# Products of 64 rows or columns made 128 wide, and the shared experts of four sequences moved beside the routed ones

## The chip, the cores and the metric

The kernel runs on one core of a Trainium2 chip. The metric is device time in microseconds (us) of one launch. The engines are PE (TensorE; its weight loads are listed as PEld), DVE (VectorE), ACT (ScalarE), POOL (GpSimd), and SP, whose queue issues most DMA transfers; POOL issues the indirect ones (gathers and scatter-adds by a list of row numbers). Each engine works through its own instructions in the order in which they were written; across engines they wait for each other by semaphores.

## The reference, cut to what matters

Two layers over 8 sequences of 512 tokens with 256 features, all in fp32; each adds its result to its input.

```python
# layer 0: an adapter per sequence (weights by language), then experts that choose tokens
h = relu(hidden @ W1[lang] + b1[lang])                 # 256 -> 64
c0 = layernorm(hidden + h @ W2[lang] + b2[lang]) * gamma[lang] + beta[lang]
G, I = top_k(swapaxes(softmax(c0 @ Wg.T)), 128)        # each of 8 experts takes 128 tokens a sequence
x = x + scatter_add(I, G * (gelu(c0[I] @ W1e + b1e) @ W2e + b2e))      # 256 -> 1024 -> 256

# layer 1: conditioning by running averages, then 64 routed experts and a shared one
md = 0.5 + sigmoid(gelu(x @ Wn1.T + bn1) @ Wn2.T + bn2)                # 256 -> 64 -> 8
c1 = layernorm((gelu(x @ Wsoma.T + ..) * sigmoid(traces(x, md) @ Wtemp.T + ..)) @ Wout.T) * gamma + beta
w, ids = top_k(softmax(c1 @ router_w.T), 8)            # of 64 experts; the first 128 tokens of each count
routed = segment_sum(w * ((silu(xe @ w_gate) * (xe @ w_up)) @ w_down)) # 256 -> 192 -> 256
sg, su = split(c1 @ ws_gate_up)                        # 192 and 192 columns
shared = (silu(sg) * su) @ ws_down
x = x + routed + shared
```

## The kernel before

**An order written by a planner.** The program is not written engine by engine. Functions add *steps* to an `Order` (L39): an engine, a planned cost in us, a function that issues the instructions, what it reads and writes, buffers that it takes from a ring (`new`), and a rank. `run` (L102) plays the steps through with the planned costs: on each engine it takes, of the steps that can begin within 0.25 us of the earliest one, that with the lowest rank. The order in which it takes them is the order in which the instructions are issued. Loads and stores are steps of SP with 0.1 us and a size; the planner lets them finish one behind the other at `RATE` = 0.19e6 bytes per us, and 2 us later. `after` holds a step back in the plan until others are done. The planned costs are no times of the chip; waits on the chip come from the tiles that instructions share.

**The stages.** `adapter(b)` (L300) for 8 sequences; `down` multiplies by the 64 columns of the gathered `aw1` (L354). `choose` makes the token lists of layer 0 on DVE. `expert(n)` (L582, down to the scatter-adds of L728) runs 8 experts for each of 4 groups of two sequences: `up` (L643), `down` (L710), then scatter-adds into `x1_rows`. `conditioning(b)` (L824) needs all experts of its group; in it `hidden` (L849) has 64 output columns and `rates` (L858) 64 rows and 8 columns, the scans are DVE's (L969, L980). `route` and `last_lists` make the token lists of the routed experts on DVE. These stages overlap: experts (rank 1000 + n) fill PE around the conditioning (rank 100 + 5 b).

**The shared experts.** `shared(b)` (L1266, rank 2000 + b, so it fills what is left of PE) reads the normed sequence back (`rc1b`, one buffer), makes gate and up in four products of 96 columns (`CH`), two at a time (L1287), multiplies silu of the one by the other (L1296 on ACT, L1299 on DVE) into `rsh`, multiplies by `wsd` in two halves of 96 rows (L1313), copies to `rob` (L1318) and stores that into `odd`, a DRAM tensor (L1326).

**The routed experts.** `pair(p)` (L1331) loads the weights of two experts, 1152 KB, into one of 6 `wfar` or 8 `wnear` buffers; pair p takes over the place of pair p - 14. `routed(e)` (L1342, rank 400 + e): a gather of 128 tokens on POOL (L1351), two transposes (L1360), scale (ACT), gate and up in one product of 384 columns (L1371), silu (L1374), a multiply (L1377), two transposes of the 192 columns (L1386; the two blocks of 128 overlap by 64), a copy (L1389), the down product as one of 128 rows (L1396) and one of 64 (L1397), a copy (L1400), and a scatter-add on POOL (L1403) into `out` for even e, into `odd` for odd e. Adds into one tensor follow each other, each waits for the landing of the one before. An add into `odd` waits for the shared sums of all eight sequences, which are stored there first; `out` holds the residual.

**The final sums.** `total(b)` (L1422) loads `odd` and `out`, adds on DVE and stores.

Each fp32 product appears as two MATMUL records.

Of the kernel before, what the change touches and what calls it, by code (L numbers as in the profile page):

```python
# [26 lines left out]
CH = 96  # L27
PAIR = 2 * 2 * (H // P) * F1 + 3 * H
FAR = 6
NEAR = 8  # L30
# [8 lines left out]
class Order:  # L39
# [3 lines left out]
    RATE = 0.19e6  # L43
# [101 lines left out]
def kernel(ctx: ExitStack, tc: tile.TileContext, d: dict, out: bass.AP):  # L145
# [64 lines left out]
        "rlr": 2, "rtk": 1, "rm8": 2, "rev": 1, "rhalf": 1, "rsecond": 1, "rws": 1, "rc1b": 1, "rsh": 1, "rsl": 1, "rob": 1,  # L210

        "wfar": FAR, "wnear": NEAR, "xe": 6, "xeT": 3, "xsl": 2, "xhe": 2, "xheT": 2, "xye": 4,
# [87 lines left out]
    def adapter(b):  # L300
# [19 lines left out]
        def row_w1():  # L320
            t = tile_of(w1, "aw1", [P, NH, A])
            nc.gpsimd.indirect_dma_start(
                out=t.rearrange("p c a -> p (c a)"), out_offset=None, in_=d["cw1"],
                in_offset=bass.IndirectOffsetOnAxis(ap=ix_w1[:, b : b + 1], axis=0),
            )
# [20 lines left out]
        pool(1.1, row_w1, new=[(w1, "aw1")], rank=rank, lag=2.5)  # L346
        pool(1.1, row_w2, new=[(w2, "aw2")], rank=rank, lag=2.5)
        pool(1.0, one, new=[(hT, "ahT")], rank=rank)
        pool(1.1, row_gains, w=[("gains", b)], rank=rank, lag=2.5)

        def down():
            ph = bank(("ph", b))
            for hc in range(NH):
                nc.tensor.matmul(ph[:A, :], V[w1][:, hc, :], V[xb][:, hc, :], start=hc == 0, stop=hc == NH - 1)  # L354
# [385 lines left out]
    def w_load():  # L740
# [14 lines left out]
        one("wn2", [HN, D1], d["wn2"], 2 * KB)  # L755
        one("bn1", [HN, 1], d["bn1"], 256)
        one_w("wn1", H, HN)
# [6 lines left out]
        one("wsd", [CH, 2, H], d["wsd"].rearrange("(c p) n -> p c n", p=CH), 192 * KB)  # L764
# [59 lines left out]
    def conditioning(b):  # L824
# [20 lines left out]
        def hidden():  # L845
            pn = bank(("pn", b))
            tile_of(K["hn"], "hn", [HN, S])
            for hc in range(NH):
                nc.tensor.matmul(  # L849
                    pn[:HN, :], W["wn1"][:, hc, :], V[K["xb"]][:, hc, :], start=hc == 0, stop=hc == NH - 1  # L850
                )

        def hidden_gelu():
            nc.scalar.activation(V[K["hn"]], V["pn", b][:HN, :], AF.Gelu, bias=W["bn1"])

        def rates():
            tile_of(K["md"], "md", [D1, S])
            nc.tensor.matmul(bank(("pm", b))[:D1, :], W["wn2"], V[K["hn"]], start=True, stop=True)  # L858
# [406 lines left out]

    def shared(b):  # L1266
        rank, soon = 2000 + b, 250 + b
        c1T, sh, ob = ("c1b", b), ("sh", b), ("ob", b)
# [6 lines left out]
        for f in range(2):  # L1275
            banks = [("sgu", b, f, k) for k in range(2)]
            sl = ("sl", b, f)
            for k in range(2):
                def into(f=f, k=k, banks=banks, sl=sl):
                    if k == 0:  # L1280
                        tile_of(sl, "rsl", [CH, S])
                        if f == 0:
                            tile_of(sh, "rsh", [CH, 2, S])
                    t = bank(banks[k], "hid")
                    f0 = k * F1 + f * CH
                    for hc in range(NH):
                        nc.tensor.matmul(  # L1287
                            t[:CH, :], W["wsgu"][:, hc, f0 : f0 + CH], V[c1T][:, hc, :],
                            start=hc == 0, stop=hc == NH - 1,
                        )  # L1290

                new = [(banks[k], "hid")] + ([(sl, "rsl")] if k == 0 else []) + ([(sh, "rsh")] if f + k == 0 else [])
                lead = [pe(2.0, into, r=[c1T, "wsgu"], new=new, rank=rank, after=lead if f + k else ())]

            def silu(banks=banks, sl=sl):
                nc.scalar.activation(V[sl], V[banks[0]][:CH, :], AF.Silu)  # L1296

            def mul(f=f, banks=banks, sl=sl):
                nc.vector.tensor_tensor(V[sh][:, f, :], V[sl], V[banks[1]][:CH, :], ALU.mult)  # L1299

            act(0.65, silu, r=[banks[0]], w=[sl], rank=soon, table="s")
            dve(0.75, mul, r=[sl, banks[1]], w=[sh], rank=45)
        for h in range(NC // 2):
            po = ("spo", b, h)

            def down(h=h, po=po):
                if h == 0:
                    tile_of(ob, "rob", [P, NC, H])
                t = bank(po, "hid").rearrange("p (c h) -> p c h", h=H)
                for c in range(2):  # L1310
                    tok = (2 * h + c) * P
                    for f in range(2):
                        nc.tensor.matmul(  # L1313
                            t[:, c, :], V[sh][:, f, tok : tok + P], W["wsd"][:, f, :], start=f == 0, stop=f == 1
# [5 lines left out]
            new = [(po, "hid")] + ([(ob, "rob")] if h == 0 else [])  # L1320
            lead = [pe(2.0, down, r=[sh, "wsd"], new=new, rank=rank, after=lead if h else ())]
            act(0.65, keep, r=[po], w=[ob], rank=soon)

        def store():

            nc.sync.dma_start(out=odd[b * S : (b + 1) * S, :].rearrange("(c p) h -> p c h", p=P), in_=V[ob])  # L1326

        load(512 * KB, store, r=[ob], w=[("sum", 1, b)], rank=rank)
# [12 lines left out]

    def routed(e):  # L1342
        rank = 400 + e
        j = e % 2
        wp_, xe, xeT, sl, he, heT, ye = (("pair", e // 2), *((k, e) for k in ("xe", "xeT", "xsl", "xhe", "xheT", "xye")))
# [20 lines left out]
        def gate_up():  # L1366
            tile_of(sl, "xsl", [P, F1])
            tile_of(he, "xhe", [P, F1])
# [7 lines left out]
        def mul():  # L1376
            nc.vector.scalar_tensor_tensor(  # L1377
                V[he], V[pgu][:, F1 : 2 * F1], V[xe][:, H + e : H + e + 1], V[sl], ALU.mult, ALU.mult
# [3 lines left out]
        def turn_h():  # L1382
            tile_of(heT, "xheT", [P, 2, C1])
            t = bank(pt)
            for f in range(2):
                nc.tensor.transpose(t[:, f * P : (f + 1) * P], V[he][:, f * (F1 - P) : f * (F1 - P) + P], ident)  # L1386
# [4 lines left out]

        def down():
            tile_of(ye, "xye", [P, H])
            t = bank(po, "res")[:, :H]
            rest = slice(P // 2, P) if j else slice(0, P // 2)
            nc.tensor.matmul(t, V[heT][:, 1 - j, :], wdn(j), start=True, stop=False)  # L1396
            nc.tensor.matmul(t, V[heT][rest, j, :], wdn(2)[rest, :], start=False, stop=True)  # L1397
# [14 lines left out]
        pe(1.6, gate_up, r=[xeT, wp_], new=[(pgu, "hid"), (sl, "xsl"), (he, "xhe")], rank=rank)  # L1412
# [4 lines left out]
        pe(1.1, down, r=[heT, wp_], new=[(po, "res"), (ye, "xye")], rank=rank)  # L1417
# [4 lines left out]
    def total(b):  # L1422
        t = ("both", b)
        rows = slice(b * S, (b + 1) * S)
        part = lambda j: V[t][:, j * NC * H : (j + 1) * NC * H]

        def get_odd():
            tile_of(t, "wfar" if b < FAR else "wnear", [P, PAIR])
            nc.sync.dma_start(out=part(1), in_=odd[rows, :].rearrange("(p c) h -> p (c h)", c=NC))  # L1429

        def get():
            nc.sync.dma_start(out=part(0), in_=out[rows, :].rearrange("(p c) h -> p (c h)", c=NC))
# [4 lines left out]
        def put():  # L1437
            nc.sync.dma_start(out=out[rows, :].rearrange("(p c) h -> p (c h)", c=NC), in_=part(0))

        load(300 * KB, get_odd, r=[("chain", 1)], new=[(t, "wfar" if b < FAR else "wnear")], rank=600 + b)  # L1440
        load(300 * KB, get, r=[("chain", 0)], w=[t], rank=610 + b)
        dve(1.3, both, w=[t], rank=600)
        load(300 * KB, put, r=[t], rank=620 + b)
# [28 lines left out]
    for p in range(E1 // 2):  # L1472
        pair(p)
    for e in range(E1):
# [8 lines left out]
def layout(inputs):  # L1483
# [4 lines left out]
    w1 = a["L0_cond_W1"].reshape(NL, NH, P, A).transpose(0, 2, 1, 3).reshape(NL * P, NH * A)  # L1488
# [10 lines left out]
    rest = np.concatenate([wdn[:, 0, : F1 - P], wdn[:, 1, P:]], axis=1)  # L1499
    wpair = np.concatenate([wgu, wdn[:, 0, F1 - P :], wdn[:, 1, :P], rest], axis=2)  # L1500
# [5 lines left out]
        "cw1": w1,  # L1506
# [11 lines left out]
        "wn1": a["L1_cond_Wn1"].T,  # L1518
        "bn1": a["L1_cond_bn1"].reshape(HN, 1),
        "wn2": a["cond_256"].T,  # L1520
# [32 lines left out]
```

## Time and profile before

| | us |
|---|---|
| median of 3 runs | 1205.87 (1204.51 to 1207.83) |
| the profiled execution | 1206.65 |
| its span, first to last instruction | 1204.9 |
| PE busy | 1068.5 (89%), 4293 products |
| DVE busy | 701.2 (58%) |
| ACT busy | 469.9 (39%) |
| POOL busy | 377.3 (31%) |
| DMA moved | 221.35 MB, 184 GB/s on average |

How to read it: the busy shares are averages over stages with different limits. The page divides the span into 40 equal slices and prints the busy share of each as a digit; the timeline lists instructions in order, merged where one line follows itself ("x4"), with start, length, and in brackets the engine's idle time before and what ended it; the windows give busy times for chosen stretches. A line number is that of the listing. A matmul's length includes the filling of the array, so the distance between the starts of two records says more of its price than its length. In the names `xe<-c_rows,ix_c` stands for "written from", and buffer numbers are left out.

### The profile page before, as it was taken

What the parts mean: (1) busy time and instruction counts of PE and PEld (TensorE: products, weight loads), DVE (VectorE), ACT (ScalarE), POOL (GpSimd) and SP (SyncE); (2) the same over time, 40 slices, a digit from 0 to 9 for tenths busy, and PEclk for the clock granted to TensorE, in tenths of its full rate; (3) what the DMA queues carried; (4) which work ended last, traced back from release to release, by engine and by line L of the source; (5) the groups of instructions that cost most, each with busy time, mean ns of one, the idle gap of its engine ahead of it and who ended that gap; (6) DMA issues with size and microseconds to landing.
All of it is one profiled execution on the core that took longest, in us unless ns stands there. A gap on an engine that the chain in (4) does not pass through costs nothing. (4 is left out here: it accounts for less than half of the span.)

```text
span 1204.9 us, 12973 instructions
## 1 busy us (share of the span) xinstructions
PE 1068.5 (89%) x4293; PEld 738.1 (61%) x4293; DVE 701.2 (58%) x1486; ACT 469.9 (39%) x998; POOL 377.3 (31%) x299
## 2 busy tenths in 40 slices
PE   4779999999999999999999999899967888899950
PEld 2457888858778667878586876345543444445530
DVE  2623180059883998946997939798575223333323
ACT  2447644443536442536434544323322212223310
POOL 6132133314232213223122221000003356778850
PEclk9669999999999999999999999999978989999985
DMA  8845466755665646557755634732193478895559
GB/s 286 285 150 184 131 194 201 204 180 175 202 196 156 209 145 210 173 140 217 227 152 162 195 91 142 295 106 70 56 371 117 129 215 230 241 245 96 90 95 386
DMA packets 89443, 221.35 MB, mean 184 GB/s; under 512 B 15185, under 2 KB 62329, under 8 KB 76961
## 3 DMA queue, kind: packets, MB, share of 16 engines
q1 hardware_dynamic: 62848, 182.73, 43.6%
q0 software_dynamic: 25472, 36.75, 16.7%
q10 hardware_dynamic: 1056, 1.05, 0.3%
q8 instruction: 34, 0.56, 0.2%
q14 instruction: 33, 0.26, 0.1%
HBM read 177.24 MB, written 47.32 MB: 186 GB/s over the span
## 5 line engine op out<-in xcount | busy, mean ns | idle before, releaser
L643 PE MATMUL hid<-exT,fw 128*128 128x256 f32 x1024 | 231.5, 381 | 1.8 <-ACT hf L653 1.8
L710 PE MATMUL res<-fw,hf 128*128 128x256 f32 x1024 | 232.6, 379 | 0.0
L643 PEld LDWEIGHTS hid<-exT,fw 128*128 128x128 f32 x1024 | 193.3, 191 | 33.4 <-issue 5.3
L710 PEld LDWEIGHTS res<-fw,hf 128*128 128x128 f32 x1024 | 191.6, 190 | 24.9 <-issue 0.5
L728 POOL DMA_INDIRECT x_rows<-y,ix x64 | 113.9, 1780 | 230.4 <-ACT y L725 219.5
L609 POOL DMA_INDIRECT xg<-c_rows,ix x64 | 68.8, 1075 | 257.1 <-PE hid L622 227.1
L653 ACT ACTIVATE hf<-hid,fb 128x256 f32<-128x256 f32 x256 | 105.1, 470 | 82.0 <-PE hid L643 81.7
L1351 POOL DMA_INDIRECT xe<-c_rows,ix_c x64 | 63.0, 984 | 202.2 <-DMA c_rows<-rlr 177.9
L980 DVE TENSOR_TENSOR_SCAN t<-alpha,u 128x512 f32<-128x512 f32 x84 | 102.8, 1224 | 2.9
L969 DVE SCALAR_TENSOR_TENSOR u<-gx,blend,mdb 128x512 f32<-128x512 f32 x128 | 95.2, 744 | 1.9 <-DMA mdb<-md_rows 0.9
L725 ACT ACTIVATE y<-y,gT 128x256 f32<-128x256 f32 x64 | 31.6, 506 | 147.8 <-DVE y L722 146.5
L1400 DVE COPY xye<-res 128x256 f32<-128x256 f32 x64 | 27.2, 425 | 81.6 <-PE res L1397 38.9
L1287 PE MATMUL hid<-rc1b,wsgu 128*96 128x512 f32 x128 | 63.3, 636 | 12.3 <-DMA rc1b<-c1T_rows 12.3
L1374 ACT ACTIVATE xsl<-hid 128x192 f32<-128x192 f32 x64 | 21.1, 330 | 128.4 <-PE hid L1371 128.4
L722 DVE TENSOR_TENSOR y<-res,fb 128x256 f32<-128x256 f32 x64 | 26.1, 418 | 69.7 <-PE res L710 69.7
L1403 POOL DMA_INDIRECT odd<-xye,ix_c x32 | 50.7, 1584 | 35.1 <-DMA odd<-rob 14.3
L982 DVE TENSOR_TENSOR tmp<-tmp,t 128x512 f32<-128x512 f32 x84 | 58.1, 692 | 2.9
L1403 POOL DMA_INDIRECT out_dram<-xye,ix_c x32 | 50.8, 1588 | 27.1 <-DVE xye L1400 9.4
L278 ACT ACTIVATE xeT<-mm,lgb 128x128 f32<-128x128 f32 x128 | 48.4, 456 | 27.8 <-PE mm L1360 25.5
L278 ACT ACTIVATE exT<-hid,gains 128x128 f32<-128x128 f32 x128 | 48.0, 457 | 28.6 <-PE hid L622 28.6
L1377 DVE SCALAR_TENSOR_TENSOR xhe<-hid,xe,xsl 128x192 f32<-128x192 f32 x64 | 26.4, 413 | 41.8 <-ACT xsl L1374 34.8
L1371 PE MATMUL hid<-wnear,xeT 128*128 128x384 f32 x128 | 50.2, 518 | 0.0
(200 smaller groups left out, 1588.3 us busy)
## 6 DMA issues: line engine op xcount, KB each, us to landing
fw<-in_fw_dram SPq DMA_DIRECT2D x64, 1024.0 KB
wfar<-in_wpair_dram SPq DMA_DIRECT2D x16, 1152.0 KB
wnear<-in_wpair_dram SPq DMA_DIRECT2D x16, 1152.0 KB
mdb<-md_rows SPq DMA_DIRECT2D x32, 512.0 KB
axb<-in_xT_dram SPq DMA_DIRECT2D x8, 512.0 KB
fb<-in_fb_dram SPq DMA_DIRECT2D x32, 128.0 KB
x_rows<-axt SPq DMA_DIRECT2D x8, 512.0 KB
c_rows<-ac SPq DMA_DIRECT2D x8, 512.0 KB
```

What stands on the lines that cost most here:

```text
L278: nc.scalar.activation(dst, src, AF.Identity, bias=gain[:, NH + hc : NH + hc + 1], scale=gain[:, hc : hc + 1])
L609: nc.gpsimd.indirect_dma_start(out=tile_of(("xg", u, b), "xg", [P, H]), out_offset=None, in_=c0_rows[b], in_offset=bass.IndirectOffsetOnAx ...
L643: nc.tensor.matmul(t[:, i, :], V[w1][:, hc, f * P : (f + 1) * P], V[exT][:, hc, :], start=hc == 0, stop=hc == NH - 1,)
L653: nc.scalar.activation(t[:, i, :], p[:, i, :], AF.Gelu_apprx_tanh, bias=fb1[:, e, f : f + 1])
L710: nc.tensor.matmul(V[res][:, :H], V[hf][:, i, j * K0 : (j + 1) * K0], V[w2][:, f, :], start=f == 0, stop=f == NF - 1,)
L728: nc.gpsimd.indirect_dma_start(out=x1_rows[b], out_offset=bass.IndirectOffsetOnAxis(ap=lists[b][0][:, e : e + 1], axis=0), in_=V[y], in_of ...
L969: nc.vector.scalar_tensor_tensor(u, V[K["gx"]][:, hc, :], W["blend"][:, hc, k : k + 1], V[mdb][:, k % 2, :], ALU.mult, ALU.mult,)
L980: nc.vector.tensor_tensor_scan(t, decay(1 + k), u, 0.0, ALU.mult, ALU.add)
L982: nc.vector.tensor_tensor(whole, whole, t, ALU.add)
L1287: nc.tensor.matmul(t[:CH, :], W["wsgu"][:, hc, f0 : f0 + CH], V[c1T][:, hc, :], start=hc == 0, stop=hc == NH - 1,)
L1351: nc.gpsimd.indirect_dma_start(out=tile_of(xe, "xe", [P, H + E1]), out_offset=None, in_=c1_rows, in_offset=bass.IndirectOffsetOnAxis(ap=ix ...
L1403: nc.gpsimd.indirect_dma_start(out=odd if j else out, out_offset=bass.IndirectOffsetOnAxis(ap=ix_c1[:, e : e + 1], axis=0), in_=V[ye], in_ ...
```

## The change

Five things, and the order that the planner makes of them.

1. *128 columns or rows.* The gathered adapter weight has a third block, a copy of the first, so that the product takes 128 columns, of which rows 64 to 127 of the result aren't used. `wn1`, `bn1`, `wn2` are padded with zeros to 128. In the routed experts the hidden tile is 256 wide, with 64 zero columns behind the 192 (even e) or ahead of them (odd e); four such tiles are kept and zeroed once (`hidden_places`), and the block of `w_down` that an expert shares with its partner holds the 64 rows of both.
2. *Shared experts in three blocks.* The 384 columns of gate and up are laid out anew as 128 of gate, 128 of up, and the last 64 of both together: three products of 128 columns for four of 96. The hidden tile `sh` is one tile for all sequences, its second half 64 zero rows and 64 used ones.
3. *Four sequences later.* For b in `LATE` (4 to 7) the place in `odd` is stored with zeros, by a step that reads nothing; the down product may come only after all of `conditioning`, its result stays in SBUF (`xob`, four buffers) and is added in `total`.
4. *Buffers.* `NEAR` 8 to 6 (so 12 pairs), `rc1b` 1 to 2, `xhe` 2 to 4.
5. *Numbers of the planner.* `RATE` 0.19e6 to 0.3e6; ranks of the adapter's gathers: weights 3 lower, gains 2 higher; 0.95 for 1.1 for the routed down product.

```diff
-NEAR = 8
+NEAR = 6
+LATE = (4, 5, 6, 7)
-    RATE = 0.19e6
+    RATE = 0.3e6
...
-            t = tile_of(w1, "aw1", [P, NH, A])
+            t = tile_of(w1, "aw1", [P, NH + 1, A])
...
-        pool(1.1, row_w1, new=[(w1, "aw1")], rank=rank, lag=2.5)
-        pool(1.1, row_w2, new=[(w2, "aw2")], rank=rank, lag=2.5)
+        pool(1.1, row_w1, new=[(w1, "aw1")], rank=rank - 3, lag=2.5)
+        pool(1.1, row_w2, new=[(w2, "aw2")], rank=rank - 3, lag=2.5)
         pool(1.0, one, new=[(hT, "ahT")], rank=rank)
-        pool(1.1, row_gains, w=[("gains", b)], rank=rank, lag=2.5)
+        pool(1.1, row_gains, w=[("gains", b)], rank=rank + 2, lag=2.5)
...
-                nc.tensor.matmul(ph[:A, :], V[w1][:, hc, :], V[xb][:, hc, :], start=hc == 0, stop=hc == NH - 1)
+                nc.tensor.matmul(ph, V[w1][:, hc : hc + 2, :].rearrange("p c a -> p (c a)"), V[xb][:, hc, :], start=hc == 0, stop=hc == NH - 1)
...
-                    pn[:HN, :], W["wn1"][:, hc, :], V[K["xb"]][:, hc, :], start=hc == 0, stop=hc == NH - 1
+                    pn, W["wn1"][:, hc, :], V[K["xb"]][:, hc, :], start=hc == 0, stop=hc == NH - 1
...
-            nc.tensor.matmul(bank(("pm", b))[:D1, :], W["wn2"], V[K["hn"]], start=True, stop=True)
+            nc.tensor.matmul(bank(("pm", b)), W["wn2"], V[K["hn"]], start=True, stop=True)
...
+    REST = slice(2 * P - F1, P)
+    sh = pools["pr"].tile([P, 2, S], F32, name="sh", bufs=1)
+    nc.gpsimd.memset(sh[: 2 * P - F1, 1, :], 0.0)
+    zeros = const.tile([P, H], F32, name="zeros")
+    nc.gpsimd.memset(zeros, 0.0)
...
+        banks = [("sgu", b, k) for k in range(3)]
+        for k in range(3):
...
+                    nc.tensor.matmul(
+                        t, W["wsgu"][:, hc, k * P : (k + 1) * P], V[c1T][:, hc, :], start=hc == 0, stop=hc == NH - 1
+                    )
+            def silu(k=k, sl=sl):
+                if k:
+                    nc.scalar.activation(V[sl][REST, :], V[banks[2]][: F1 - P, :], AF.Silu)
+                else:
+                    nc.scalar.activation(V[sl], V[banks[0]], AF.Silu)
+            def mul(k=k, sl=sl):
+                at = slice(0, P) if k == 1 else REST
+                nc.vector.tensor_tensor(sh[at, k - 1, :], V[sl][at, :], V[banks[k]][at, :], ALU.mult)
+            new = [(banks[k], "hid")] + ([(sl, "rsl")] if k != 1 else [])
+            lead = [pe(2.0, into, r=[c1T, "wsgu"], new=new, rank=rank, after=lead if k else ())]
+            if k != 1:
+                act(0.65, silu, r=[banks[k]], w=[sl], rank=soon, table="s")
+            if k:
+                dve(0.75, mul, r=[sl, banks[k]], w=[("sh", k - 1)], rank=45)
...
-            lead = [pe(2.0, down, r=[sh, "wsd"], new=new, rank=rank, after=lead if h else ())]
+            lead = [pe(2.0, down, r=[("sh", 0), ("sh", 1), "wsd"], new=new, rank=rank, after=(lead if h else last_tokens if b in LATE else ()))]
...
-            nc.sync.dma_start(out=odd[b * S : (b + 1) * S, :].rearrange("(c p) h -> p c h", p=P), in_=V[ob])
-        load(512 * KB, store, r=[ob], w=[("sum", 1, b)], rank=rank)
+            src = zeros.unsqueeze(1).to_broadcast([P, NC, H]) if b in LATE else V[ob]
+            nc.sync.dma_start(out=odd[b * S : (b + 1) * S, :].rearrange("(c p) h -> p c h", p=P), in_=src)
+        load(512 * KB, store, r=() if b in LATE else [ob], w=[("sum", 1, b)], rank=80 if b in LATE else rank)
...
+    def hidden_places():
+        def fill():
+            for k in range(4):
+                t = V["he", k] = tile_of(("he", k), "xhe", [P, 2 * P])
+                nc.gpsimd.memset(t[:, F1:] if k % 2 == 0 else t[:, : 2 * P - F1], 0.0)
+        pool(1.0, fill, w=[("he", k) for k in range(4)], rank=399, after=last_tokens)
...
-                nc.tensor.transpose(t[:, f * P : (f + 1) * P], V[he][:, f * (F1 - P) : f * (F1 - P) + P], ident)
+                nc.tensor.transpose(t[:, f * P : (f + 1) * P], V[he][:, f * P : (f + 1) * P], ident)
...
-            rest = slice(P // 2, P) if j else slice(0, P // 2)
-            nc.tensor.matmul(t, V[heT][:, 1 - j, :], wdn(j), start=True, stop=False)
-            nc.tensor.matmul(t, V[heT][rest, j, :], wdn(2)[rest, :], start=False, stop=True)
+            nc.tensor.matmul(t, V[heT][:, j, :], wdn(j), start=True, stop=False)
+            nc.tensor.matmul(t, V[heT][:, 1 - j, :], wdn(2), start=False, stop=True)
...
+        laid = lambda x: x[rows, :].rearrange("(c p) h -> p c h" if b in LATE else "(p c) h -> p c h", **as_laid)
+        def shared_too():
+            nc.vector.tensor_add(part(1), part(1), V["ob", b])
...
+        load(300 * KB, get_odd, r=[("chain", 1)], new=[(t, "wfar" if b < FAR else "wnear")], w=[(t, 1)], rank=600 + b)
+        if b in LATE:
+            dve(1.3, shared_too, r=[("ob", b)], w=[(t, 1)], rank=600)
+        load(300 * KB, get, r=[t, ("chain", 0)], w=[(t, 0)], rank=610 + b)
+        dve(1.3, both, r=[(t, 1)], w=[(t, 0)], rank=600)
+        load(300 * KB, put, r=[(t, 0), t], rank=620 + b)
```

## The prediction

> **What bounds the kernel now.** I read the busy slices first, then the timeline of POOL and of PE over the routed experts, the chain of waits, and the windows. The slices:
>
> ```profile
> PE   4779999999999999999999999899967888899950
> POOL 6132133314232213223122221000003356778850
> ```
>
> One digit is 30.1 us. PE is at 9 from 90 to about 745 us (dense experts mixed with the conditioning of sequences 0 to 5); then DVE carries the conditioning of 6 and 7 (to 877) and the last token lists (to 917); from 917.64 (first gather of L1351) to the last scatter-add at 1167.04 come the 64 routed experts, where POOL climbs to 8; the last 35 us are the final sums, with PE and POOL idle. In 90 to 745 all waits of PE add up to 15.7 us (L1017 6.4, L909 3.1, xr 2.8, L643 1.8, L1113 1.6), so there PE sets the pace.
>
> The routed experts, steady part, PE and POOL timelines (start, us, group; in brackets the idle time before it and what ended it):
>
> ```profile
> 1106.56 0.59 PE L1396 MATMUL res<-wnear,xheT 128*128 128x256 f32 x2
> 1107.09 0.70 PE L1397 MATMUL res<-wnear,xheT 64*128 64x256 f32 x2
> 1107.71 1.56 PE L1371 MATMUL hid<-wnear,xeT 128*128 128x384 f32 x4
> 1109.11 0.38 PE L1386 MATMUL mm<-ident,xhe 128*128 128x128 f32 x2
> ...
> 1105.60 0.99 POOL L1351 DMA_INDIRECT xe<-c_rows,ix_c  x1 [0.30 <-PE mm L1386]
> 1106.89 1.59 POOL L1403 DMA_INDIRECT out_dram<-xye,ix_c  x1 [0.30 <-issue]
> 1108.79 0.99 POOL L1351 DMA_INDIRECT xe<-c_rows,ix_c  x1 [0.30 <-issue]
> ```
>
> The reader is to see two things. A 64-row product is dear on PE: the four records of one down product take 1.15 us (1106.56 to 1107.71), while 24 plain records of 256 columns (L710, 98.22 to 103.41) take 0.216 us each, 0.864 for four. So 0.29 goes in and around L1397, and 0.11 more on L1371 behind it (1.40 against four times the usual 0.323). And POOL never rests: 0.99 + 0.30 + 1.59 + 0.30 = 3.18 us an expert, all gaps 0.30, while PE goes round in 3.13 (two experts in 6.27). PE is nearly full, but POOL is the floor.
>
> Before that part POOL waits:
>
> ```profile
> 953.74 0.95 POOL L1351 DMA_INDIRECT xe<-c_rows,ix_c  x1 [0.30 <-issue]
> 969.01 1.63 POOL L1403 DMA_INDIRECT odd<-xye,ix_c  x1 [14.33 <-DMA odd<-rob]
> ...
> 1024.05 7.41 DMA out_dram<-xye,ix_c
> ...
> 1162.54 3.78 DMA odd<-xye,ix_c
> ```
>
> The first pair, POOL's timeline: the scatter-add of expert 1 stands at the head of POOL until the shared sums of sequence 7 are stored in `odd` at 969; by then three adds are done since 931.31. The last two, from the chain of waits: an add takes 7.41 us to land while pair weights stream, 3.78 when they have ended. The windows show that streaming as the DMA share (the columns: PE, PEld, DVE, ACT, POOL busy, PE clock, DMA share, GB/s):
>
> ```profile
> 1017.00:1075.00 58.00, 51.42 (x195) 27.98 (x193) 18.54 (x49) 17.75 (x49) 41.28 (x32) 1.00 0.89 250
> 1075.00:1155.00 80.00, 78.82 (x306) 44.72 (x306) 30.12 (x77) 27.70 (x77) 65.05 (x50) 1.00 0.61 109
> ```
>
> From 1017.15 to 1075.02 POOL's timeline has 16 steps from add to add, 3.62 us each; afterwards 3.19.
>
> **The change, part by part.** The sum is made on the profiled execution: span 1204.9, time 1206.65, so 1.75 lies around the span; the median shown, 1205.87, is 0.8 lower.
>
> *Conditioning and adapter products made 128 wide (L354, L849, L858).* No instruction is added; PE streams as many columns. What goes is the toll around them. At 772.48 four records of L849 take 1.87 us until the next start against 4 x 0.429 = 1.72 (0.15), and the record before and the group behind them pay 0.09 and 0.11; L858 at 780.44 pays 0.09, its neighbours 0.09 and 0.11. That is 0.65 a sequence, six sequences in the PE-bound stretch: 3.9. L354 at 86.86 and 90.64: 1.86 against 1.72, the L643 group between 1.92 against 1.73, some 0.33 each, three of them there: 1.0. Together **-4.9**. Before 81 us, and for 6 and 7, the cover is DVE (top-k 41 to 66, scans 775 to 855): nothing. Bounds: 0 if the toll follows from something else, -6.5 if all eight count. The gathers of `cw1` grow from 128 to 192 floats a row, the constants by some 0.2 MB (0.7 us at 285 GB/s), and on POOL the rows of `gains` go behind those of the weights; the first gather, for which PE waits until 11.58, stays the first: 0, with 0.7 as the bound.
>
> The Trainium skill, "TensorEngine Tiling (Array Packing)", section Tiling Modes, says that a change of tiling mode drains TensorE; this agrees with the 0.09 to 0.11 around each such product, whereas the same page's use of packing, two 64-row products at once, would halve them instead. By the drain alone, twice per routed expert and no exposed weight load, its gain would be about 0.2 us, not 0.4.
>
> *The routed down product with 128 rows.* Same four records, 0.29 + 0.11 = 0.4 us less of PE per expert, 64 times 25 us of PE time. Against POOL's 3.18 this is worth nothing in the steady part: PE goes to 2.74 and waits. If POOL were not there it would be 25. Taken: 0 by itself. The four memsets of `hidden_places` (512 floats took 0.52) stand on POOL where it waits for the lists (idle 177.9 us before 917.64): 0.
>
> *Shared experts in three blocks.* 16 records of 0.429 become 12: 1.72 us of PE a sequence, 13.7 for eight. They run from 727 on, as filler behind the conditioning's DVE work. ACT (two of 0.59) and DVE (two of 0.67) stay two each. Taken: 0.
>
> *Four sequences beside the routed experts.* Zeros go into `odd` for 4 to 7 without a reader's wait, rank 80. By the order of ranks they leave SP after the last weight (30.54 now), ahead of the stores of x and the loads for adapters 3 and 4: 2 MB at the 285 GB/s of those slices, 7.4 us later. Cover: PE idles 12.15 us before 66.60 waiting for the top-k (L549). Taken 0; without the cover +7.4. Their PE work, 12 x 0.429 + 16 x 0.216 = 8.6 us a sequence, may begin its second half only after the last conditioning (877). From there to 917 PE is 24.2 of 40 us busy with the sequences left today, and the second input buffer lets the load of sequence 6 go ahead of the pair weights (today 9.25 us of PE wait at 906). I place 4 to 6 there, 7 there or among the first experts.
>
> So the wait of 14.33 us and what follows from it go. First add at 931.3, as now. Then two paces. While weights stream, 3.62: with 12 pair buffers for 14, pair 31 is fetched when pair 19 is used up, so about 42 adds; then 3.19. 931.3 + 41 x 3.62 + 22 x 3.19 = 1150, against 1167.0: **-17**. Bounds: 63 x 3.19 from 931.3 gives 1132 (-35); 3.66, the pace of 969.01 to 1075.02 (29 steps), for all 63 gives 1162 (-5). I take the middle case, because the stream is the same 1.15 MB for two experts, and 0.89 of DMA is close to full.
>
> The skill's "TensorE: Matmul & The Clock Gate", part on the HAM clock gate, speaks against thinner PE work: an idle window of some 3.4 us halves the clock. The trace has it: after an idle 5.61 us, L1396 took 1.22 for two records at 979.65, and 0.70 at full clock. By that rule an expert would cost 2 x 2.74 = 5.5 us in cold windows; with the clock at 1.00 in both windows above, at PE busy shares of 0.89 and 0.99, and waits of under 0.5 us an expert, I count none.
>
> *Final sums.* Four DVE adds (1.23 each) wait for the first read of `odd`; behind them on DVE stand only the final adds, which wait for the second read: hidden, 4.9 if not. Sequences 4 to 7 move in rows of 1 KB for 4 KB: packets of 46 ns against 159 for 4 KB in the trace's DMA records, 4 x 46 - 159 = 25 ns, 96 such packets an engine for 6.3 MB: **+2.4**; bounds 0 and 4.9 + 2.4.
>
> *The order.* RATE only moves instructions among each other. Bounds: PE's 15.7 us of waits in 90 to 745 gone, or doubled. The list stage too: L1165 waits 4.11 us behind shared work at 881.5, which may go, and four more multiplies of 0.6 may stand among the top-k steps. Taken 0 for both.
>
> **Sum.** -4.9 - 17 + 2.4 = -19.5: span 1185.4, time 1187.2; on the median's scale 1186.4. I say **1186**.
>
> **The rivals.** *POOL is never held up:* chance 0.18. For it: PE has 0.4 us more slack, and fair shares of DMA may suffice. Against: adds of 7.4 us in two alternating chains cannot go at 3.19. Time 1186.4 - 18 = 1168.
> *The stream holds the whole stage (3.66 to the end):* 0.15. For it: two pair buffers less. Against: 3.19 from 1075 on now. Time 1186.4 + 12 = 1198; with half of the order's cost it is no change.
> *The shared work is put behind the routed experts:* 0.15, the slower side. Its rank, 2000, is the last, and the planner books 3.35 us of PE an expert (0.4, 1.6, 0.4, 0.95) against 3.2 of POOL, so its PE never looks free. Then up to four times 8.6 = 34 us of PE, alone, lie between the last expert and the sums: 1186 + 34 = 1220. It decides from 2.3 sequences on (19.5 / 8.6). Against: the 16 idle us of PE before 917.
> That the toll does not vanish is within the first bounds (+4.9).
>
> **How the numbers follow.** The forecast has 0.52, with its own range 1176 to 1196. A change under 0.3% (3.6 us) can't be told from none. Faster takes the forecast, the first rival and 0.10 of the second: 0.80; same 0.05; slower 0.15. The range goes from 1164 (first rival with its share of the order) to 1205: some 0.1 lies above it and 0.06 below.
>
> **What would show it.** Right: L1397 starts 0.22 us a record and L1371 after it 0.32; no POOL wait for `odd`; adds 3.6 apart until the pair loads end near 1080, then 3.19; the dense stretch ends some 5 us earlier. Wrong: L1287's successors after the last down product; POOL gaps of 0.30 throughout (too slow a forecast); PE waits in 90 to 745 over 16 us (too fast).

## The result, and the profile after

The changed kernel takes **1209.83 us** (median of 20 runs, 1204.62 to 1216.34) against 1202.99 for the kernel before (20 runs beside it): ratio **1.0065**, 95% interval 1.0046 to 1.0085. The forecast of 1186 us, 0.9835 of the 1205.87 shown, was on the wrong side. The profiled execution took 1209.93, its span is 1208.1.

Where the two profiled executions part, in us from the start of each span:

| stage | before | after | forecast |
|---|---|---|---|
| first dense down product (L710, now L711) | 96.1 | 104.0 | 96.1 |
| last dense down product | 735.1 | 749.6 | 730.2 |
| from there to the first gather of the routed experts | 182.5 | 182.5 | 182.5 |
| first gather to last scatter-add | 249.4 | 234.8 | 232.4 |
| last scatter-add to the end | 37.9 | 41.2 | 40.3 |

The second half did what was forecast, to 3.3 us. The loss lies in the first: 14.5 us later where 4.9 earlier was expected. (The 182.5 of the third row hides two changes that cancel: from the last dense product to the last routing transposes 140.0 us for 147.0, from there to the first gather 42.5 for 35.5.) The slices of the page (30.2 us a digit) show it only faintly, for PE is busy all through:

```profile
PE   4789999899999999999899999899976987788840
POOL 6132233214232223232123222000001676677850
```

PE has 8s where it had 9s in the dense stretch, and its list of waits between 90 and 760 us (us in total, times, longest) starts with two that were small before (xr 2.8 and hf 1.8 in 90 to 745):

```profile
PE mm L263 <- DMA xr<-x_rows: 14.9, 4, 4.8
PE hid L644 <- ACT hf L654: 7.4, 6, 2.3
```

All waits of PE there are 34.1 us, for 15.7 before: the sign of a forecast that is too fast, which the prediction had set at over 16. That looked like the whole answer; the experiments show that it is not.

The routed experts, steady part, timeline of PE after (start, us, group, idle time before):

```profile
1104.95 0.65 PE L1415 MATMUL res<-wnear,xheT 128*128 128x256 f32 x2
1105.44 0.59 PE L1416 MATMUL res<-wnear,xheT 128*128 128x256 f32 x2
1105.88 1.45 PE L1392 MATMUL hid<-wnear,xeT 128*128 128x384 f32 x4
1107.17 0.38 PE L1407 MATMUL mm<-ident,xhe 128*128 128x128 f32 x2
```

The down product takes 0.93 us (1104.95 to 1105.88) where it took 1.15, and the product behind it 1.29 for 1.40. POOL's timeline after:

```profile
945.03 1.62 POOL L1422 DMA_INDIRECT out_dram<-xye,ix_c  x1 [0.30 <-DVE xheT L1410]
...
948.26 1.59 POOL L1422 DMA_INDIRECT odd<-xye,ix_c  x1 [0.30 <-DVE xheT L1410]
...
1100.08 1.60 POOL L1422 DMA_INDIRECT out_dram<-xye,ix_c  x1 [0.30 <-issue]
1101.98 0.99 POOL L1373 DMA_INDIRECT xe<-c_rows,ix_c  x1 [0.30 <-issue]
1103.28 1.60 POOL L1422 DMA_INDIRECT odd<-xye,ix_c  x1 [0.30 <-issue]
```

The wait of 14.33 us at the head of POOL is gone: the first add into `odd` follows the first into `out` by 3.2 us. Later the step is 3.20 (1100.08 to 1103.28): POOL is the floor, as said. In the chain of waits an add lands as slowly as before or more slowly while the weights stream (three pieces take 8.18, 9.74 and 10.55 us, where 7.41 was the longest before), and as fast once they have ended:

```profile
1013.75 7.45 DMA out_dram<-xye,ix_c
...
1166.93 3.74 DMA odd<-xye,ix_c
```

The windows (PE, PEld, DVE, ACT, POOL busy, PE clock, DMA share, GB/s) differ from those before in PE's share and in the clock:

```profile
1017.00:1075.00 58.00, 43.73 (x169) 29.53 (x170) 16.26 (x43) 15.89 (x44) 37.20 (x29) 0.91 0.82 230
1075.00:1155.00 80.00, 70.49 (x297) 47.25 (x296) 27.43 (x72) 27.80 (x74) 61.77 (x48) 0.98 0.61 123
```

The clock was 1.00 in both. PE is less busy (43.73 for 51.42), and some of its products run at half clock.

### The profile page after: what moved, and what is told of

It reads as the page before. It is cut to its first block, busy times and chain, and to the rows that moved or that the text cites. A ratio compares the mean times of both kernels' runs of the same rounds, so it can differ in the third digit from the quotient of the medians.

```text
span 1208.1 us, 12950 instructions
## 1 busy us (share of the span) xinstructions
PE 1041.6 (86%) x4261; PEld 763.2 (63%) x4261; DVE 706.6 (58%) x1490; ACT 470.0 (39%) x996; POOL 383.2 (32%) x305
## 5 line engine op out<-in xcount | busy, mean ns | idle before, releaser
L644 PE MATMUL hid<-exT,fw 128*128 128x256 f32 x1024 | 234.9, 385 | 7.4 <-ACT hf L654 7.4
L711 PE MATMUL res<-fw,hf 128*128 128x256 f32 x1024 | 234.3, 382 | 0.0
L711 PEld LDWEIGHTS res<-fw,hf 128*128 128x128 f32 x1024 | 194.1, 192 | 26.8 <-issue 1.4
L729 POOL DMA_INDIRECT x_rows<-y,ix x64 | 119.8, 1872 | 263.6 <-ACT y L726 256.9
L1392 PE MATMUL hid<-wfar,xeT 128*128 128x384 f32 x144 | 56.9, 523 | 0.0
L1178 DVE MAX8 rhalf<-rev 128x8 f32<-128x512 f32 x64 | 44.4, 693 | 1.7
```

The source lines that it names most:

```text
L644: nc.tensor.matmul(t[:, i, :], V[w1][:, hc, f * P : (f + 1) * P], V[exT][:, hc, :], start=hc == 0, stop=hc == NH - 1,)
L711: nc.tensor.matmul(V[res][:, :H], V[hf][:, i, j * K0 : (j + 1) * K0], V[w2][:, f, :], start=f == 0, stop=f == NF - 1,)
L729: nc.gpsimd.indirect_dma_start(out=x1_rows[b], out_offset=bass.IndirectOffsetOnAxis(ap=lists[b][0][:, e : e + 1], axis=0), in_=V[y], in_of ...
L1392: nc.tensor.matmul(t[:, : 2 * F1], V[xeT][:, hc, :], wgu()[:, hc, :], start=hc == 0, stop=hc == NH - 1)
```

## The experiments

Ratios are to the kernel before on the same chip, with 95% intervals; 1% is 12 us. Stage lengths are from one profiled execution of each kernel; the routed stage varies by some 3 us between kernels that leave it alone (246.8 to 252.8 us in the kernel before and the four variants of it that don't touch the routed or shared experts). The planner's `RATE` was suspected first: 0.3e6 lets it think that loads land sooner than they do, so PE is written to stand before loads that are late.

**`RATE` back at 0.19e6 in the changed kernel.**

```diff
-    RATE = 0.3e6
+    RATE = 0.19e6
```

> The changed kernel with RATE back at 0.19e6, nothing else. Theory of the order: the stretch of dense experts lost its time because the planner believed loads to land sooner; then PE's waits in it fall from 34.8 us to some 16, the last dense down product starts at 731 to 736 us instead of 749.6, the routed stage keeps its shorter length (235 us from first gather to last add), and the time falls by some 15 to 20 us, to 1190 to 1195. Theory of the width: padded products or the other ranks of the adapter's gathers cost the time; then the dense stretch still ends near 750 and the time stays near 1209.

1207.45 us, ratio 1.0021 (0.9996 to 1.0045). The waits of PE in the dense stretch fall to 21 us, but the first dense down product still starts at 104.0 and the last at 743.8. Of the gap to the forecast (0.9835) most is there with the old `RATE`: the theory fell as the main cause.

**`RATE` 0.3e6 in the kernel before.**

```diff
-    RATE = 0.19e6
+    RATE = 0.3e6
```

> The kernel before with RATE 0.3e6, nothing else. Theory of the order: the last dense down product moves from 735 to some 750 to 755 us, waits of PE for xr appear there, and the time rises by 12 to 20 us. Theory of the width: no change, within 4 us.

1214.91 us, ratio 1.0081 (1.0054 to 1.0108). It costs the kernel before 0.8%, less than expected, and its waits for xr are those of the changed kernel (14.5 us). Its last scatter-add is 6.4 us later; half of that, 3.0, is there at the first gather, and in the routed stage POOL's wait for `odd` is 19.91 us in place of 14.33.

**Only the 128-wide conditioning and adapter products** (the gathered third block, `wn1`, `bn1`, `wn2` padded) in the kernel before.

```diff
-                nc.tensor.matmul(ph[:A, :], V[w1][:, hc, :], V[xb][:, hc, :], start=hc == 0, stop=hc == NH - 1)
+                nc.tensor.matmul(ph, V[w1][:, hc : hc + 2, :].rearrange("p c a -> p (c a)"), V[xb][:, hc, :], start=hc == 0, stop=hc == NH - 1)
```

> The kernel before with the products of the adapter and of the conditioning (L354, L849, L858) 128 wide, nothing else. The prediction's own step: the toll of some 0.65 us a sequence and 0.33 an adapter goes, the last dense down product starts 3 to 5 us earlier, and the time falls by 3 to 5 us. Theory of the width: it rises by 5 us or more.

1202.05 us, ratio 0.9979 (0.9949 to 1.001): at most a few us, and the interval takes in no change at all. In its profile the last dense down product starts 1.1 us earlier (734.0 for 735.1).

**Only the routed down product of 128 rows** in the kernel before.

```diff
-            nc.tensor.matmul(t, V[heT][:, 1 - j, :], wdn(j), start=True, stop=False)
-            nc.tensor.matmul(t, V[heT][rest, j, :], wdn(2)[rest, :], start=False, stop=True)
+            nc.tensor.matmul(t, V[heT][:, j, :], wdn(j), start=True, stop=False)
+            nc.tensor.matmul(t, V[heT][:, 1 - j, :], wdn(2), start=False, stop=True)
```

> The kernel before with the routed down product as two of 128 rows (zeroed hidden tiles, weights laid out anew), nothing else; gate and up still wait for the transposes two experts back. POOL is the floor: PE has 0.4 us an expert less to do, POOL's steady pace stays 3.19 us an expert, and the time changes by 0 to -4 us. If PE were the floor the time would fall by 0.4 us for each of some 40 experts, 15 us or more.

1206.31 us, ratio 1.0033 (1.0006 to 1.006). The routed stage is 248.8 us for 249.4: 25 us less of PE time are worth nothing there.

What was left was the start. In SP's queue the four zero stores stand in front of the adapters' stores and loads (30.80 to 34.88 us in the kernel with `RATE` 0.19e6). So they were moved, and also tried alone.

**Zero stores behind the last adapter, `RATE` 0.19e6.**

```diff
-        load(512 * KB, store, r=() if b in LATE else [ob], w=[("sum", 1, b)], rank=80 if b in LATE else rank)
+        load(512 * KB, store, r=() if b in LATE else [ob], w=[("sum", 1, b)], rank=rank, after=last_adapter if b in LATE else ())
```

> The changed kernel with RATE 0.19e6 and the four zero stores of odd set behind the last adapter instead of in front of the adapters' stores. Theory that the zero stores push the adapters' loads back at the start: the first dense up product goes from 90.2 us back to about 82, the last dense down from 743.8 to about 735, and the rest keeps its lengths (186.6 to the first gather, 239 of routed experts, 41 to the end): about 1199. Rival, that something else in the change delays the start (the adapter gathers, the longer constants): first dense up product still at 90, about 1207.

1199.01 us, ratio 0.9935 (0.9905 to 0.9966). First dense up product at 82.6, last dense down at 733.1: as the theory has it.

**The same with `RATE` 0.3e6 kept.**

> The changed kernel, RATE 0.3e6 kept, with the zero stores set behind the last adapter. If the zero stores are most of the loss and RATE little: first dense down product some 2 to 8 us earlier than 104.0, about 1202 to 1204. If RATE is the loss: still some 1207 to 1210, with the waits of PE for xr and hf at 20 us and more between 90 and 760.

1201.97 us, ratio 0.9973 (0.9948 to 0.9999). With the four stores moved, the changed kernel is no longer slower: 1.0065 to 0.9973, 0.92% or 11 us. The waits for xr and hf are still there (14.7 and 7.0 us), so they were not what cost most.

**Zero stores alone, added to the kernel before.**

```diff
+        load(512 * KB, store, w=[("sum", 1, b)], rank=80)
```

> The kernel before with four zero stores of 512 KB into odd added at rank 80 (the stores of the shared sums overwrite them later). Theory that these stores alone hold up the start: the first dense up product moves from 81.6 to about 90 and the whole run with it, 1209 to 1211. Rival, that 2 MB hide behind the top-k as predicted: first dense up product at 82, about 1203.

1210.6 us, ratio 1.006 (1.003 to 1.0089); first dense up product at 90.2 for 81.6. PE's timeline around the top-k of layer 0, first of the kernel before, then of this one:

```profile
50.81 3.65 PE L354 MATMUL mm<-axb,aw 128*64 128x512 f32 x8
66.60 0.28 PE L554 MATMUL mm<-ident,bestf 32*128 32x32 f32 x1 [12.15 <-DVE bestb L549]
```

```profile
67.80 0.31 PE L554 MATMUL mm<-ident,bestf 32*128 32x32 f32 x1 [15.64 <-DVE bestf L549]
...
68.41 4.53 PE L354 MATMUL mm<-axb,aw 128*64 128x512 f32 x5
```

The adapters' products (L354), which filled a part of PE's wait for the top-k, now stand behind the instruction that waits. PE idles 15.64 us in place of 12.15 and does them afterwards. It is the only difference in PE's order: the other instructions of PE, and all of DVE's, follow each other as in the kernel before. The changed kernel with `RATE` 0.19e6 shows the same: 15.73 us of idle time, and eight products of L355 behind it. Is that traffic, or the order as written?

**The same stores at the same place, entered in the plan with 1 KB each.** All 4293 of PE's instructions come out in the order of the kernel before.

```diff
+        load(1 * KB, store, w=[("sum", 1, b)], rank=80)
```

> The kernel before with the same four zero stores at the same place of SP's queue, but entered in the planner with 1 KB each, so that PE's written order is that of the kernel before, instruction for instruction. If the loss of the run with full entries came from the planned time (PE's products set behind the top-k's transposes): first dense up product at 81.6 to 83, about 1203 to 1205. If the 2 MB of traffic themselves hold up the adapters' loads: first dense up product at 88 to 90, about 1210.

1204.26 us, ratio 0.9999 (0.9964 to 1.0033); first dense up product at 82.6. Its timeline:

```profile
51.93 3.65 PE L354 MATMUL mm<-axb,aw 128*64 128x512 f32 x8
67.73 0.28 PE L554 MATMUL mm<-ident,bestf 32*128 32x32 f32 x1 [12.15 <-DVE bestb L549]
```

The 2 MB moved as in the run before (the four stores leave SP from 31.43 us on, for 31.54 there) and cost nothing that can be measured. The price was the **planned** time: four times 512 KB at 0.19e6 bytes per us are 11 us by which the planner took the adapters' loads to be late, so it wrote their products behind the wait.

In the changed kernel as it stands, with `RATE` 0.3e6, the loss at the start looks different. There L355's eight products stand ahead of the wait with and without the early zero stores. What comes later is DVE's top-k. DVE's timeline, first of the changed kernel, then of the one with late zero stores:

```profile
56.47 0.18 DVE L443 RECIPROCAL ars<-asd 128x4 f32<-128x4 f32 x1 [3.02 <-ACT asd L439]
68.34 0.21 DVE L550 COPY bestr<-best 32x128 f32<-32x128 f32 x1
```

```profile
60.20 0.15 DVE L443 RECIPROCAL ars<-asd 128x4 f32<-128x4 f32 x1
63.86 0.21 DVE L550 COPY bestr<-best 32x128 f32<-32x128 f32 x1
```

A step of an adapter's layer norm (L443) stands in the middle of the top-k and waits 3.02 us for ACT; the top-k's result is there 4.5 us later (68.34 for 63.86). Moving the stores took away their planned time and their early traffic together, and in this kernel the two were not tried apart.

Next, the list stage. From the last routing transposes to the first gather the kernel before needs 35.5 us (882.1 to 917.6), the changed one 42.5 (889.6 to 932.1). DVE's timeline in the changed kernel:

```profile
893.12 0.68 DVE L1179 MATCH_REPLACE8 rev<-rhalf,rev 128x512 f32<-128x512 f32 x1
895.06 0.69 DVE L1306 TENSOR_TENSOR sh<-rsl,hid 128x512 f32<-128x512 f32 x1 [1.27 <-PE hid L1324]
895.67 0.69 DVE L1178 MAX8 rhalf<-rev 128x8 f32<-128x512 f32 x1
```

The top-k step at 895.67 stands behind a multiply of a shared expert, which waits 1.27 us for a product of the sequence before (L1324): `sh` is now one tile for all sequences.

**The multiplies of sequences 4 to 7 behind the lists, two sequences really among the routed experts** (with late zero stores, `RATE` 0.19e6).

```diff
-        rank, soon = 2000 + b, 250 + b
+        rank, soon = 410 + 6 * (b - 5) if b in LATE else 2000 + b, 250 + b
...
-                dve(0.75, mul, r=[sl, banks[k]], w=[("sh", k - 1)], rank=45)
+                dve(0.75, mul, r=[sl, banks[k]], w=[("sh", k - 1)], rank=390 if b in LATE else 45)
```

> As the kernel with RATE 0.19e6 and late zero stores, but the multiplies of the shared experts of sequences 4 to 7 get rank 390 and their products ranks 404 to 422, so that two of these sequences really fall among the routed experts and no multiply stands among the last top-k steps. Theory that these multiplies and DVE's waits for their products lengthened the list stage: from the last routing transposes to the first gather 39.5 falls to about 35, and 4 to 5 us come off: about 1195. Rival, that the products cost their full 8.6 us a sequence among the routed experts: the routed stage grows by 10 to 17 us, about 1205 to 1212.

1191.76 us, ratio 0.9897 (0.985 to 0.9943). The list stage falls from 39.6 to 35.4 us. The routed stage is 233.8 us (237.4 without): the shared products fill gaps of PE and don't lengthen it. Four runs were made of this kernel, and its interval overlaps with that of the kernel that it changes (0.9905 to 0.9966).

**`LATE` empty** (with `RATE` 0.19e6; all sums stored in `odd`).

```diff
-LATE = (4, 5, 6, 7)
+LATE = ()
```

> The changed kernel with RATE 0.19e6 and LATE empty: all eight sequences stored in odd as before, no zero stores, rows of 4 KB in the final sums for all. Against the kernel with late zero stores (1199.0) the theory that the late sequences give the routed stage its gain says: POOL's wait for odd of 10 to 14 us is back, the routed stage 249 in place of 237, the final sums some 3 us shorter, about 1207. Rival, that the stage is shorter for another reason (the full-height products, the hidden buffers): routed stage 237 without them too, about 1196.

1198.75 us, ratio 0.9941 (0.991 to 0.9972): the theory fell, the rival held. POOL's timeline:

```profile
933.09 1.61 POOL L1422 DMA_INDIRECT out_dram<-xye,ix_c  x1 [1.94 <-DVE xye L1419]
...
936.30 1.59 POOL L1422 DMA_INDIRECT odd<-xye,ix_c  x1 [0.30 <-DVE xheT L1410]
```

No wait for `odd`, a routed stage of 234.6 us, and not one sequence is late. Something else in the change lets the last shared sums land in time.

**One buffer for the shared input, `LATE` empty.**

```diff
-"rc1b": 2
+"rc1b": 1
```

> The kernel with LATE empty (1198.75), with one buffer for the shared experts' input in place of two. Theory that the second buffer lets all shared sums be stored before the first add of an odd expert: with one, the load of sequence 7 waits again, its products fall among the first routed experts, POOL waits for odd 8 us or more, the routed stage is 243 to 250 in place of 234.6: about 1206 to 1210. Rival, that the three blocks alone are enough: no such wait, about 1199.

1204.71 us, ratio 0.9987 (0.9965 to 1.0008). The wait is back, though the profile names no releaser for it:

```profile
963.52 1.62 POOL L1422 DMA_INDIRECT odd<-xye,ix_c  x1 [11.04 <-issue]
```

The last shared down product of this run ends at 957.6 and its sum is stored at 958.23, so the wait is taken to be for `odd`; the routed stage is 251.0 us.

**Two buffers in the kernel before**, with `NEAR` 7 to make room.

```diff
-NEAR = 8
+NEAR = 7
...
-"rc1b": 1
+"rc1b": 2
```

> The kernel before with two buffers for the shared experts' input (and one near pair buffer less, which makes the room). If the buffer alone is the cause: POOL's wait of 14.33 us for odd falls below 4, the routed stage from 249.4 to about 238, about 1193. If both the buffer and the fewer records are needed: the last shared sums still land behind the first adds, the wait is 6 us or more, 1200 to 1206.

1197.61 us, ratio 0.993 (0.9901 to 0.9958). The wait shrinks from 14.33 to 5.20 us, the routed stage from 249.4 to 243.1:

```profile
957.98 1.63 POOL L1403 DMA_INDIRECT odd<-xye,ix_c  x1 [5.20 <-DMA odd<-rob]
```

That lies between the two cases of the expectation. The buffer alone takes 9 of the 14 us of waiting; in the changed kernel with `LATE` empty, which has the three blocks beside it (and the other parts of the change), the wait is gone; with one buffer that kernel gains nothing on this stage. Four late sequences with one buffer were not run.

Then the two last parts. **Rows of 4 KB for all final sums**, added to the run with the two sequences among the routed experts:

```diff
+                    cols = slice(2 * h + c, S, NC) if b in LATE else slice(tok, tok + P)
-                            t[:, c, :], sh[:, f, tok : tok + P], W["wsd"][:, f, :], start=f == 0, stop=f == 1
+                            t[:, c, :], sh[:, f, cols], W["wsd"][:, f, :], start=f == 0, stop=f == 1
```

> The kernel with two sequences among the routed experts (1191.8), with the shared down products of sequences 4 to 7 taking every fourth token as their columns, so that the final sums move rows of 4 KB for all sequences. Theory of the 1 KB rows: the time from the last scatter-add to the end falls from 40.8 to about 38, and 2 to 3 us come off: about 1189. Rival, that the four extra adds set the length of the final sums or that columns at a stride slow the weight loads: no gain or a loss, 1192 or more.

**1188.96 us**, ratio **0.9872** (0.9824 to 0.9921), the fastest of all by its median. From the last scatter-add to the end it is 39.0 us for 40.8. The medians differ by 2.8 us as the theory has it, but the intervals overlap.

**The same with `RATE` 0.3e6.**

> As the kernel of the run before, with RATE 0.3e6. If RATE by itself costs what it seemed to cost the kernel before (8 to 10 us): about 1198. If it costs the little by which the changed kernel with 0.19e6 stood below the changed kernel: about 1190 to 1192.

1189.45 us, ratio 0.9873 (0.9827 to 0.9918): here `RATE` costs nothing that can be measured. In its profile PE still waits 14.4 us for xr; the dense stretch from the first down product to the last is 639.3 us for 638.5, the start 8.7 later, and from the last dense product to the first of the routing transposes it needs 141.1 for 145.2.

**Only sequences 6 and 7 late.**

```diff
-LATE = (4, 5, 6, 7)
+LATE = (6, 7)
```

> The best kernel so far (1188.96) with only the sequences 6 and 7 added late; 4 and 5 are stored in odd as 0 to 3 are. Theory that what matters is only that no shared work stands before the lists or in front of the first odd add: 1188 to 1190, and two adds of 1.23 us less ahead of the final sums. Rival, that the stores of 4 and 5 land late and POOL waits for odd: 1192 to 1198.

1193.28 us, ratio 0.9903 (0.988 to 0.9926). The time falls into the rival's range, but its wait isn't there: POOL doesn't wait for a stored sum. The interval overlaps with that of four late sequences, so whether the other two are better late isn't settled.

## Why the prediction was wrong

**Zero stores: the step that failed.** "Taken 0; without the cover +7.4." The cover was real: in the kernel before the 2 MB cost nothing by themselves (0.9999), though the adapter load behind them was issued 4.9 us later (36.78 for 31.93), where 7.4 had been reckoned. What was not looked at is that the order is written from planned times. A step "without a reader's wait" still advances the planner's DMA clock by 11 us at 0.19e6 (7 at 0.3e6), and so changes the order in which the steps behind it are written. Moved behind the adapters, the changed kernel gains 0.92% (11 us), at the other `RATE` 0.86% (1.0021 to 0.9935). With `RATE` 0.3e6 the profiles show 6.4 us of it at the first dense down product (104.0 to 97.6) and 7.0 more up to the last (749.6 to 736.2); how those 7.0 arise was not taken apart, and the profiled execution with late stores was the fastest of its ten (1194.73 us, median 1201.97), so a part of the 13.4 may be scatter.

**"*The order.* RATE only moves instructions among each other … Taken 0 for both."** The second part that failed. Of its bounds, the doubled waits came true (15.7 to 34.1 us), yet the time follows them only in part: `RATE` costs 0.81% in the kernel before, about 0.4% with late zero stores (0.9973 against 0.9935, intervals that overlap), nothing in the last version. In the kernel before a part of it is the longer wait for `odd`, which the last version doesn't have. The list stage: its 4.11 us wait for L1165 did go (0.60 after), but six multiplies among the list steps, where three stood before, and their waits took more. Setting them behind the lists, with two sequences' products among the routed experts, gave 4.2 us of that stage and 0.38% in the medians.

**Four sequences late: −17 was right in size and wrong in cause.** The 14.33 us wait went, and the routed stage got 14.6 us shorter. But the prediction gave that to the late sums and 0 to the three blocks; without any late sum the stage is as short, and with one input buffer besides it isn't. In the changed kernel not one of the late sequences lay among the routed experts: their last shared product ends at 929.6, ahead of the first gather at 932.1. So the late sums weren't needed. Without them the gain hangs on the second input buffer, which the prediction named in half a sentence; whether late sums with one buffer would have given it too, no run shows. That the size came out right is luck as far as the cause goes.

**The two paces.** 3.62 while weights stream was too fast: the first 37 adds, up to the last pair load, go at 3.88. Two things differ there from the kernel before: adds that land in 8.18 to 10.55 us stand in the chain, and the clock in 1017 to 1075 was 0.91, for which the prediction counted nothing. Which of them made the pace slower was not tried. From the first add to the last it took 221.9 us for 218.6 forecast.

**128-wide products: −4.9.** Measured −0.2% (−0.5 to +0.1), some 2.5 us; in its profile the dense stretch ends 1.1 us earlier where 4.9 were expected. The toll itself went: in the changed kernel four records of L355 take 1.71 us until the next start (73.95 to 75.66), for 1.86 before.

**Routed down product: 0** was right for the stage (248.8 for 249.4); the time rose by 0.3% (1.0006 to 1.006), which these runs don't explain. **Final sums: +2.4** was 3.3, and 1.8 of that came back with rows of 4 KB.

**The rivals.** Shared work behind the routed experts did not happen. Neither did the other two: steps of 3.20 after the stream, 3.88 in it.

The gap from 0.9835 to 1.0065 is 2.30%. Zero stores 0.92, `RATE` 0.38 and the multiplies 0.38 make 1.68%, or 20 us; the toll (2.4 us), the pace (3.3) and the final sums (0.9) would make most of the rest. This is an account by medians and single profiles: each of the two steps of 0.38 lies within overlapping intervals. The version with these parts set right measured 0.9872 (0.9824 to 0.9921), near the forecast, but it is another kernel, and its shorter routed stage doesn't need the late sums to which the forecast gave it.

## What to carry to other kernels

Where the order of instructions is written from planned times, a step that costs the chip nothing still costs what it makes the planner believe; compare the written order of each engine, not only the resources. An instruction that waits on an in-order engine is paid by what is written behind it. When a wait goes, ask which of the edits took it away by putting back one at a time: here the part that was made for it could be left out, and without that part a second buffer could not.

## What was not expected of the hardware

The clock fell to half after a wait of 2.21 us and had stayed up after a longer one. PE's timeline in the changed kernel shows waits of 2.08 us (at 1013.86) and 2.44 (at 1022.10) with products at full clock behind them, and then:

```profile
1030.11 0.95 PE L1415 MATMUL res<-wfar,xheT 128*128 128x256 f32 x2 [2.21 <-DVE xheT L1410]
1030.85 1.06 PE L1416 MATMUL res<-wfar,xheT 128*128 128x256 f32 x2
1031.71 2.51 PE L1392 MATMUL hid<-wfar,xeT 128*128 128x384 f32 x4
```

The granted clock from 1030 to 1034 is 0.57, and four records of L1392 take 2.51 us for 1.45. "TensorE: Matmul & The Clock Gate" of the Trainium skill, Part 1, gives an idle window of about 3.4 us as the condition and says that the window runs freely. No single wait here is that long. But the place of a wait matters. In the trace's record the granted clock falls at 999.70 and 1030.42 and rises at 1003.12 and 1033.84, all of them whole multiples of 3.41 us apart. Windows laid on this grid, one for each of the three waits and the one that follows (columns as before):

```profile
1009.94:1013.36 3.42, 1.84 (x8) 0.88 (x6) 0.31 (x1) 0.77 (x3) 1.65 (x2) 1.00 1.05 347
1020.18:1023.60 3.42, 1.50 (x6) 1.25 (x7) 1.41 (x4) 0.00 (x0) 1.60 (x1) 1.00 0.52 147
1027.01:1030.42 3.41, 1.20 (x4) 0.49 (x3) 1.08 (x3) 0.33 (x1) 1.41 (x2) 1.00 0.97 304
1030.42:1033.84 3.42, 3.42 (x8) 2.23 (x7) 0.42 (x1) 0.00 (x0) 2.81 (x3) 0.50 0.56 73
```

The waits of 2.08 and 2.44 us are each cut in two by the grid and leave PE busy for 1.84 and 1.50 us of the window; that of 2.21 lies in one window and leaves 1.20, and the next window runs at half clock. From 941 to 1078 us it is so throughout: the clock falls after the five windows in which PE was busy for 0 to 0.39 of the time, and stays up after all other windows at full clock, which have 0.44 and more. The fixed grid agrees with the page; an idle window in full was not needed here. Elsewhere in the run some falls follow busier windows, so this orders the stretch shown and is no rule for the rest.
